# A four-layer graph network on one core: the last layer's attention by seven half-block products, and layernorm's small work moved to GpSimd

## The chip, the core and the metric

The kernel runs on one core of a Trainium2 chip. The core has a matrix engine (TensorE; PE in the profile, with its weight loads as PEld), a vector engine (DVE), an activation engine (ACT), GpSimd (POOL), and SyncE (SP), which here only issues DMAs. Each engine works through its own queue in order; semaphores connect the queues. Matmuls write to PSUM, which GpSimd can't reach; everything else lies in SBUF. The metric is device time in microseconds, a median of several runs.

## The reference

There are 32 graphs of 512 nodes with 256 features each, and four layers, each of the form x = x + layer(relu(layernorm(x)), adj). All four are attentions over the graph's neighbours with different scores. The norm of every layer, and the last layer, which the change rewrites:

```python
h = jnp.maximum(_layernorm(x, axis=-1), 0.0)      # mean, variance, 1/sqrt(v + eps)
...
h = jnp.matmul(feat, W)
Ax = jnp.matmul(h, a_1); Ay = jnp.matmul(h, a_2)
A_xy = jnp.matmul(jnp.matmul(h, a_12), jnp.swapaxes(h, 1, 2))
e = jax.nn.leaky_relu(jnp.swapaxes(Ax, 1, 2) + Ay + A_xy, negative_slope=ALPHA)
e = jnp.where(adj > 0, e, NEG_INF)
attention = jax.nn.softmax(e, axis=-1)
h_out = jnp.matmul(feat, W_1) + jnp.matmul(jnp.matmul(attention, feat), W_2)
return jax.nn.elu(h_out)
```

Layers 1 and 2 have scores of rank one (a leaky sum of a row term and a column term), layer 0 a full product of scores and two convolutions.

## The kernel before, in words

**Tiling.** A graph's 512 nodes are four tiles of 128 partitions. `x`, `y`, `w` and the like are [128, 4, 256] float32, one "page" of 4 KB per partition; there are 34 pages, 8 PSUM banks, 5 buffers for values `v` ([128, 4, 259]), and room for six graphs in flight. Weights of an attention (`e{l}_0` and `e{l}_1`) are two pages of [128, 2, 512]: node tiles 0, 1 and 2, 3 on the partitions, all 512 receivers along the free axis.

**Order.** Nothing loops on the chip. Each piece of work is registered with `op(engine, cost, after, emit, keys...)`: its engine, how long it holds that engine and until when its result lasts (the pair of ns at the top of the file), what it follows, the code that issues it, and the pages and banks that it uses. `Plan.order` then plays all 32 graphs on a model of the engines: whenever an engine is free, it takes the ready operation with the earliest due time, and due times follow from a distance between graphs (one for most, one for the last few), of which the pair with the shortest replay is taken. The instructions are issued in this order, so every engine's queue is fixed in advance and interleaves several layers of several graphs. `SLACK` stretches the costs that the plan reckons with: 1.03 on DVE and ACT, 1.5 on GpSimd.

**Layernorm** (`normed`, lines 552 to 607), for each pair of tiles: DVE takes each tile's statistics (557) and aggregates them to mean and variance (558), adds epsilon (561); GpSimd raises the result to the power -0.5 (564); DVE forms -mean times that (567); ACT normalizes each tile and clips it (571). The tile is then split into 16-bit planes (576), transposed by DMA (579) and joined by ACT (591).

**Products in seven.** Most products of 2 x 2 blocks are already done by seven half-size products in place of eight (`seven`, line 619): bank `p` collects products 1, 6, 7 and 4 one after another, with a copy by ACT or DVE after each, and bank `q` (or the other half of `p`) products 2, 5 and 3, each of which is added to the copy by DVE. Nine such groups run per graph: banks f0, v0, q0, v1, v2, v3, f3, s3, w3. The sums of blocks that they need are formed on DVE (`block_sums`).

**Attention** (`attend`, line 745) is not among them: for two node tiles at a time it runs over the four tiles c of weights, one matmul (758) of 128 x 128 weights against a row of `v`, 257 to 259 columns wide; the last column or columns hold ones, so the product's last column is the sum of the weights. In layer 3 the width is 259. What follows reads the bank: for layer 3 a reciprocal of the sum (1120) and one DVE instruction that scales the product and adds the term `w3` (1125), then the elu and the residual (1131 to 1137) and the store, issued by GpSimd (1154).

**Weights of layers 1 to 3.** Layers 1 and 2 (`leaky_exp_t`): for each of the four tiles ACT forms the leaky sum (732) and the exponential (735), and DVE applies the mask (956, 986). Layer 3: leaky on ACT (1086), a subtraction of the row's shift on DVE (1089), the exponential on ACT (1092), each tile by tile.

Of the kernel before, what the change touches and what calls it, by code (L numbers as in the profile page):

```python
# [38 lines left out]
V_STATS, V_XN, V_TINY, V_TWO = (525.0, 610.0), (322.0, 407.0), (80.0, 165.0), (255.0, 340.0)  # L39
# [3 lines left out]
G_POW, G_STORE = (800.0, 850.0), (900.0, 900.0)  # L43
V_SUM, V_BLOCK = (334.0, 425.0), (790.0, 880.0)
# [162 lines left out]
def kernel(  # L207
# [55 lines left out]
        "w": (pair, F32, "page"), "crest": ([P, 4, N], BF16, "page"),  # L263
        "hs": ([P, 4, N // 2], F32, "page"), "fs": ([P, 4, N // 2], F32, "page"),
# [3 lines left out]
        "st": ([P, NT, 6], F32, None), "mv": ([P, NT, 2], F32, None), "sT": ([P, P], F32, "sT"),  # L268
        "ve": (stat, F32, None), "rstd": (stat, F32, None), "rs": (stat, F32, None), "off": (stat, F32, None),
# [205 lines left out]
    def graph(b, adj_before, x_before):  # L475
# [76 lines left out]
        def normed(l, xs):  # L552
# [3 lines left out]
            def stats(t):  # L556
                nc.vector.bn_stats(T[f"st{l}"][:, t, :], T["x"][:, t, :])  # L557
                nc.vector.bn_aggr(T[f"mv{l}"][:, t, :], T[f"st{l}"][:, t, :])  # L558

            def variance(g):  # L560
                nc.vector.tensor_scalar(T[f"ve{l}"][:, two(g)], T[f"mv{l}"][:, two(g), 1], EPS, None, ALU.add)  # L561

            def root(g):
                nc.gpsimd.tensor_tensor(T[f"rstd{l}"][:, two(g)], T[f"ve{l}"][:, two(g)], mhalf[:, two(g)], ALU.pow)  # L564

            def offset(g):
                nc.vector.scalar_tensor_tensor(T[f"off{l}"][:, two(g)], T[f"mv{l}"][:, two(g), 0], -1.0,  # L567
                                               T[f"rstd{l}"][:, two(g)], ALU.mult, ALU.mult)
# [26 lines left out]
            for g in range(NT // 2):  # L595
# [4 lines left out]
                a = op("V", V_TINY, [a, d], partial(variance, g))  # L600
                r = op("G", G_POW, [a], partial(root, g))
                r = op("V", V_TINY, [r], partial(offset, g))
# [14 lines left out]
        def seven(key, cost, after, keys, work, write, add, beside=0):  # L617
# [16 lines left out]
            def times(x, bank, start, fresh, *wait):  # L634
                return op("PE", cost, after(x) + list(wait), lambda: work(x, T[bank][:, start:], fresh), bank, *keys)
# [69 lines left out]
        def leaky_exp_t(l, vs, sign):  # L705
# [28 lines left out]
            def exp(c):  # L734
                nc.scalar.activation(e(l, c), e(l, c), AF.Exp, scale=sign)  # L735
# [349 lines left out]
        def leaky3(c):  # L1085
            nc.scalar.activation(e(3, c), e(3, c), AF.Prelu, bias=zero, alpha=ALPHA)  # L1086
# [114 lines left out]
```

## Time and profile before

| | us |
|---|---|
| median of 3 runs (2353.06 to 2353.42) | 2353.38 |
| span of the profiled execution | 2353.1 |
| PE busy (granted clock 0.999) | 2328.9 |
| PEld busy | 1992.0 |
| DVE busy | 2099.7 |
| ACT busy | 1719.9 |
| POOL busy | 254.2 |
| layer attention's matmuls, line 758, 4096 instructions, busy | 1017.7 |

The profile is of one execution. Its own time is known only as the span, from the first to the last instruction of the program; it is 0.3 us under the median. Busy time is the union of an engine's instructions. A group's row gives line, engine, operation, the names written and read, the shapes and the count; then busy us, the mean ns of one, and the idle us of the engine just before them, with what ended it. A row of the waits names who waited, for whom, the us in total, how often, and the longest. A row of the chain or of the timeline gives the start in us, the length in us, and what it is. Float32 matmuls appear as two instructions each, and matmuls overlap: one instruction lasts about 165 ns longer than the distance to the next one.

### The profile page before, as it was taken

How to read it: one execution, taken by the hardware profiler on the slowest of the kernel's cores; microseconds unless marked ns; L12 is line 12 of the kernel's file. 1: busy time of each engine (PE TensorE's matmuls, PEld its weight loads, DVE VectorE, ACT ScalarE, POOL GpSimd, SP SyncE). 2: the span in 40 equal slices, each digit the busy share in tenths (PEclk: the TensorE clock that was granted, in tenths of full speed). 3: DMA queues.
4: the chain of work that ended last, by engine and by line, in shares of the span. 5: the costliest groups of instructions: out<-in, count | busy, mean ns of one | idle time of the engine just before them, and what ended most of it. 6: DMA issues, size and time to landing. Idle time of an engine off the chain costs nothing.

```text
span 2353.1 us, 37623 instructions
## 1 busy us (share of the span) xinstructions
PE 2328.9 (99%) x12374; PEld 1992.0 (85%) x12374; DVE 2099.7 (89%) x6060; ACT 1719.9 (73%) x3421; POOL 254.2 (11%) x316
## 2 busy tenths in 40 slices
PE   8999999999999999999999999999999999999998
PEld 5789888888888888888898888888888888888887
DVE  8788899989889898898998889989898988987998
ACT  5677778767787677786777877677776778667874
POOL 3000101111011111011110010100101000010110
PEclk9999999999999999999999999999999999999999
DMA  7431233323333332333323334233343333321221
GB/s 192 106 78 28 57 79 79 88 66 83 72 75 84 78 83 66 70 88 90 82 58 74 80 85 90 54 82 70 88 91 68 86 68 73 86 54 33 55 49 42
DMA packets 429859, 178.26 MB, mean 76 GB/s; under 512 B 384128, under 2 KB 401664, under 8 KB 429664
## 3 DMA queue, kind: packets, MB, share of 16 engines
q1 hardware_dynamic: 424288, 157.51, 31.2%
q0 software_dynamic: 5232, 18.23, 2.4%
q8 instruction: 97, 1.59, 0.3%
q14 instruction: 98, 0.80, 0.1%
q10 hardware_dynamic: 144, 0.13, 0.0%
HBM read 67.64 MB, written 16.89 MB: 36 GB/s over the span
## 4 chain that ended last, share of the span: by engine, by line
PE 94%; DVE 4%; DMA 1%; ACT 1%; issue 0%; POOL 0%; DVEq 0%; ACTq 0%
PE bank_a L758 36%; PE bank_z L918 9%; PE bank_s3p L1040 5%; PE bank_o L936 4%; PE bank_q0p L874 4%; PE bank_f3p L783 4%; PE bank_w3p L809 4%; PE bank_v0p L809 4%; PE bank_f0p L783 4%; PE bank_s3q L1040 3%; PE bank_q0q L874 3%; PE bank_v1p L809 2%; PE bank_v3p L809 2%; PE bank_v2p L809 2%; PE bank_v3q L809 2%; PE bank_v1q L809 2%
## 5 line engine op out<-in xcount | busy, mean ns | idle before, releaser
L758 PE MATMUL bank_a<-v,e 128*128 128x258 f32 (+2 forms) x4096 | 1017.7, 381 | 0.9 <-DVE e L956 0.9
L758 PEld LDWEIGHTS bank_a<-v,e 128*128 128x128 f32 x4096 | 744.1, 190 | 108.9 <-issue 18.2
L591 ACT COPY hT<-planesT 128x512 uint16<-128x512 uint16 x508 | 377.8, 769 | 93.9 <-DMA planesT<-planes 93.2
L564 POOL TENSOR_TENSOR rstd<-ve,mhalf 128x2 f32<-128x2 f32 x256 | 216.0, 863 | 1732.3 <-DVE ve L561 1599.4
L571 ACT ACTIVATE xn<-x,off,rstd 128x256 f32<-128x256 f32 x512 | 278.0, 593 | 39.8 <-DVE off L567 38.9
L918 PE MATMUL bank_z<-e,y 128*128 128x512 f32 x512 | 240.8, 593 | 0.0
L557 DVE BATCH_NORM_STATS2 st<-x 128x6 f32<-128x256 f32 x512 | 210.5, 411 | 3.8 <-DMA x<-in_x_dram 3.8
L576 DVE COPY planes<-xn 128x512 uint16<-128x512 uint16 x380 | 156.4, 420 | 17.3 <-DMA planesT<-planes 10.2
L882 ACT ACTIVATE e<-e 128x512 f32<-128x512 f32 x124 | 77.8, 629 | 121.9 <-DVE e L893 61.8
L732 ACT ACTIVATE e<-row,v 128x512 f32<-128x512 f32 x224 | 156.6, 719 | 0.8 <-DMA row<-row 0.7
L735 ACT ACTIVATE e<-e 128x512 f32<-128x512 f32 x256 | 157.1, 630 | 0.0
L918 PEld LDWEIGHTS bank_z<-e,y 128*128 128x128 f32 x512 | 92.7, 190 | 64.9 <-issue 60.5
L695 ACT COPY v<-bank_v1p 128x258 f32<-128x258 f32 x128 | 47.7, 373 | 120.0 <-PE bank_v1p L809 119.3
L936 PE MATMUL bank_o<-w_sb,zT 128*128 128x256 f32 x512 | 118.5, 379 | 0.2 <-ACT zT L922 0.2
L1047 DVE SCALAR_TENSOR_TENSOR e<-bank_s3p,v,mask 128x256 f32<-128x256 f32 x256 | 111.0, 475 | 8.4 <-PE bank_a L758 4.4
L558 DVE BATCH_NORM_AGGREGATE mv<-st 128x2 f32<-128x6 f32 x512 | 93.2, 182 | 17.5
L936 PEld LDWEIGHTS bank_o<-w_sb,zT 128*128 128x128 f32 x512 | 95.8, 190 | 12.8 <-ACT zT L922 0.6
L664 DVE TENSOR_TENSOR hs<-hT,hs 128x256 f32<-128x256 f32 x254 | 105.1, 414 | 1.1
L667 DVE TENSOR_TENSOR hs<-hT 128x512 f32<-128x512 f32 x127 | 86.6, 682 | 14.5 <-ACT hT L591 14.3
L1086 ACT ACTIVATE e<-e,zero 128x512 f32<-128x512 f32 x128 | 88.2, 721 | 12.9 <-DVE crest L1064 11.4
L885 DVE TENSOR_TENSOR e<-bank_q0p,mask 128x512 f32<-128x512 f32 x124 | 84.5, 682 | 13.8 <-PE bank_q0p L874 12.3
L1089 DVE TENSOR_TENSOR e<-e,crest 128x512 f32<-128x512 f32 x128 | 85.9, 682 | 8.3 <-ACT crest L1083 8.1
(202 smaller groups left out, 4891.3 us busy)
## 6 DMA issues: line engine op xcount, KB each, us to landing
adj<-in_adj_dram SPq DMA_DIRECT2D x128, 256.0 KB
x<-in_x_dram SPq DMA_DIRECT2D x31, 512.0 KB
out_dram<-y POOLq DMA_DIRECT2D x31, 512.0 KB, 3.6
row<-row SPq DMA_DIRECT2D x56, 256.0 KB
planesT<-planes SPq DMA_TRANSPOSE x508
codeT<-code SPq DMA_TRANSPOSE x124
crest<-crest SPq DMA_TRANSPOSE x64
row<-sT SPq DMA_DIRECT2D x56, 2.0 KB
```

What stands on the lines that cost most here:

```text
L557: nc.vector.bn_stats(T[f"st{l}"][:, t, :], T["x"][:, t, :])
L564: nc.gpsimd.tensor_tensor(T[f"rstd{l}"][:, two(g)], T[f"ve{l}"][:, two(g)], mhalf[:, two(g)], ALU.pow)
L571: nc.scalar.activation(T[f"xn{l}"][:, t, :], T["x"][:, t, :], AF.Relu, bias=T[f"off{l}"][:, t : t + 1], scale=T[f"rstd{l}"][:, t : t + 1])
L591: nc.scalar.copy(bits[:, :, :, t * P : (t + 1) * P], T[f"planesT{l}_{t}"].rearrange("p (b c) n -> p b c n", b=2))
L735: nc.scalar.activation(e(l, c), e(l, c), AF.Exp, scale=sign)
L758: nc.tensor.matmul(T[key][:, : LEAD + H + 1 - lead], e(l, c)[:, t * P : (t + 1) * P], T[f"v{l}"][:, c, lead:], start=(c == 0), stop=(c == ...
L783: nc.tensor.matmul(p[:, : N // 2], w[:, x - 1, :], right(x), start=fresh, stop=True, skip_group_check=True)
L809: nc.tensor.matmul(p[:, j * k : (j + 1) * k], right(x)[:, j * P : (j + 1) * P], w[:, x - 1, :], start=fresh and j == 0, stop=True, skip_gr ...
L874: nc.tensor.matmul(p[:, j * N // 2 : (j + 1) * N // 2], right(x)[:, j * P : (j + 1) * P], left(x), start=fresh and j == 0, stop=True, skip ...
L918: nc.tensor.matmul(T[f"bank_z{k}"], T["y0"][:, c, k * P : (k + 1) * P], e(0, c), start=(c == 0), stop=(c == NT - 1))
L936: nc.tensor.matmul(T[key][:, j * H : (j + 1) * H], T["zT"][:, k, t * P : (t + 1) * P], w1_sb[:, k, :], start=(k == 0), stop=(k == HC - 1))
L1040: nc.tensor.matmul(p[:, j * N // 2 : (j + 1) * N // 2], left(x)[:, j * P : (j + 1) * P], right(x), start=fresh and j == 0, stop=True, skip ...
```

## The change

**Layernorm.** The aggregate and the three small instructions on DVE go. GpSimd forms variance, root and offset from the two half-row statistics that `bn_stats` leaves, in ten instructions on [128, 2]:

```diff
             def stats(t):
                 nc.vector.bn_stats(T[f"st{l}"][:, t, :], T["x"][:, t, :])
-                nc.vector.bn_aggr(T[f"mv{l}"][:, t, :], T[f"st{l}"][:, t, :])
...
+            def moments(g):
+                st = T[f"st{l}"][:, two(g), :]
+                gap, total, var, rstd, off = (T[f"{n}{l}"][:, two(g)] for n in ("gap", "sum", "var", "rstd", "off"))
+                gp = nc.gpsimd
+                gp.tensor_tensor(gap, st[:, :, 1], st[:, :, 4], ALU.subtract)
+                gp.tensor_tensor(var, st[:, :, 2], st[:, :, 5], ALU.add)
+                gp.tensor_tensor(gap, gap, gap, ALU.mult)
+                gp.tensor_scalar(var, var, 1.0 / H, EPS, ALU.mult, ALU.add)
+                gp.tensor_scalar(gap, gap, 0.25, None, ALU.mult)
+                gp.tensor_tensor(var, var, gap, ALU.add)
+                gp.tensor_tensor(rstd, var, mhalf[:, two(g)], ALU.pow)
+                gp.tensor_tensor(total, st[:, :, 1], st[:, :, 4], ALU.add)
+                gp.tensor_scalar(total, total, -0.5, None, ALU.mult)
+                gp.tensor_tensor(off, total, rstd, ALU.mult)
...
-                a = op("V", V_TINY, [a, d], partial(variance, g))
-                r = op("G", G_POW, [a], partial(root, g))
-                r = op("V", V_TINY, [r], partial(offset, g))
+                r = op("G", G_CHAIN, [a, d], partial(moments, g))
```

**Weights two tiles at once.** In layers 1 and 2 the exponential and the mask, in layer 3 the leaky pass, the subtraction and the exponential each take a whole page of [128, 2, 512] in one instruction where they took [128, 512]. For example:

```diff
-        def masked1(c):
-            nc.vector.scalar_tensor_tensor(e(1, c), T["codeT"][:, c, :], TINY, e(1, c), ALU.max, ALU.min)
+        def masked1(g):
+            nc.vector.scalar_tensor_tensor(T[f"e1_{g}"], T["codeT"][:, two(g), :], TINY, T[f"e1_{g}"], ALU.max, ALU.min)
```

**Layer 3's attention.** In graphs 0 to 26 (`b < B - 5`) `attend` is replaced by `attend_by_seven`, which forms the block sums of weights (four DVE instructions of 512 columns) and of values (one of 512, two of 256, and a small memset on GpSimd) and hands them to `seven`. Each of the seven products is four matmuls (2 x 2 tiles) of 128 columns; products 3 and 5 take 130, so that the sum of the weights comes out in the last one. New pages: `es3_0`, `es3_1`, `vs3`.

```diff
+            def weights_one():
+                nc.vector.tensor_tensor(T[far][:, 0], weight(1, 0), weight(1, 1), ALU.add)
...
+            def weights_two():
+                nc.vector.tensor_tensor(weight(1, 0), weight(0, 0), T[far][:, 0], ALU.add)
...
+            def work(x, p, fresh):
+                a, b_ = left[x](), right[x]()
+                k = b_.shape[2]
+                for i in range(2):
+                    for j in range(2):
+                        nc.tensor.matmul(p[:, i * WIDE : i * WIDE + k], a[:, j, i * P : (i + 1) * P], b_[:, j, :],
+                                         start=fresh and i == j == 0, stop=True, skip_group_check=True)
...
+            def write(i, f, key, start, after):
+                return op("A", A_HALF, after, lambda: nc.scalar.copy(block(i, f), part(key, start)[:, :, :HALF]), key, f"y{l}")
+
+            def add(i, f, key, start, after):
+                def emit():
+                    nc.vector.tensor_tensor(block(i, f), block(i, f), part(key, start)[:, :, :HALF], ALU.add)
+                    if f == 1:
+                        nc.vector.reciprocal(T[f"rs{l}"][:, two(i)], part(key, start)[:, :, WIDE - 1])
...
-        us = attend(3, es, vs, fourth)
+        if b < B - 5:
+            cs = attend_by_seven(3, [es[0], es[2]], list(vs[0]), [row])
+            us = [op("V", V_PSUM, c + [wb[0, t // 2], wb[1, t // 2]], partial(both_terms_of, t), "y3", "w3")
+                  for t, c in enumerate(cs)]
+        else:
+            us = attend(3, es, vs, fourth)
```

The product is copied to and summed in `y3` in SBUF (four ACT copies, three DVE adds), and `both_terms_of` scales it there and adds `w3`. The plan's costs change with it: statistics alone 340 ns, the GpSimd chain 2200 (lasting 2250), 1024-column passes 1140 on DVE and 960 to 1050 on ACT. `seven` now takes its keys per product.

## The prediction

> **What bounds the kernel now.** I read the page's engine shares first, then three stretches of one graph each from the middle, then who made the tensor engine wait, then the chain that ended last.
>
> ```profile
> span 2353.1 us, 37623 instructions
> PE 2328.9 (99%) x12374; PEld 1992.0 (85%) x12374; DVE 2099.7 (89%) x6060; ACT 1719.9 (73%) x3421; POOL 254.2 (11%) x316
> 602.00:674.00 72.00, 72.00 (x386) 61.97 (x386) 64.36 (x187) 53.48 (x109) 8.06 (x9) 1.00 0.29 64
> 1178.00:1250.00 72.00, 72.00 (x387) 61.98 (x386) 64.29 (x187) 53.17 (x109) 8.04 (x9) 1.00 0.31 63
> ...
> PE bank_n L584 <- ACT xn L571: 8.8, 1, 8.8
> PE bank_f3p L783 <- ACT fa L793: 2.0, 1, 2.0
> PE bank_w3p L809 <- ACT w L1108: 1.9, 1, 1.9
> ```
>
> In the stretches the columns after the length are PE, PEld, DVE, ACT and POOL busy. PE is busy in all 72 us at a granted clock of 1.00; DVE has 7.6 us left per graph, ACT 18.5, POOL 64. The waits of PE are one at the very start (8.8 us) and two of about 2 us near the end; the others add up to under 5 us. So between head and tail **a graph takes as long as the sum of its matmuls**, and PE time taken out is time taken out, as long as nothing else comes late. Busy matmuls overlap (381 ns each in the groups), so their price is read from the chain of waits, where a piece runs to the start of the next:
>
> ```profile
> 622.10 0.45 PE bank_v0p L809 x4
> 649.22 1.74 PE bank_a L758 x8
> 2315.17 1.34 PE bank_w3p L809 x12
> 2334.79 7.87 PE bank_a L758 x36
> ```
>
> A 259-column matmul (last line, layer 3) costs 7.87/36 = 218.6 ns; a 128-column one, with its own weight load, 1.34/12 = 111.7 ns (0.45/4 = 112 in the first).
>
> **The change, part by part.** (a) *Attention of layer 3, graphs 0 to 26.* Each f32 matmul is two instructions, as the group row shows (4096 for 2048 calls). Out go 16 calls = 32 instructions of 259 columns: 32 x 218.6 = 6995 ns. In come 7 products x 4 calls x 2 = 56 instructions, 40 of 128 and 16 of 130 columns. The 130-column form is not in the trace: below it lies 111.7 (128 columns), above it 113.5 (111.7 plus two columns at 218.6/259 = 0.84). I take 112.5, between them. 40 x 111.7 + 16 x 112.5 = 6268. That is 0.73 us per graph, **27 x 0.73 = 19.6 us**. Bounds: with 111 for all 21.0; with 113.5 for all 17.3. Weight loads rise by 24 per graph, but the 128-column products of the v and w banks have the same one load per 128 columns and run at the 112 used.
>
> The seven products go one after another through bank p, each waiting for ACT's copy (about 0.37 us), and bank q for DVE's adds. What hides this is the work of other graphs and layers: nine such chains per graph run in the trace already (f0, v0, q0, v1, v2, v3, f3, s3, w3), and PE still has no gap. Cover gone, a chain would show some six waits of 0.5 us, 3 us per graph.
>
> (b) *DVE.* The rows:
>
> ```profile
> L557 DVE BATCH_NORM_STATS2 st<-x 128x6 f32<-128x256 f32 x512 | 210.5, 411 | 3.8 <-DMA x<-in_x_dram 3.8
> L558 DVE BATCH_NORM_AGGREGATE mv<-st 128x2 f32<-128x6 f32 x512 | 93.2, 182 | 17.5
> L561 DVE TENSOR_SCALAR ve<-mv 128x2 f32<-128x2 f32 x256 | 37.6, 159 | 0.0
> L567 DVE SCALAR_TENSOR_TENSOR off<-mv,rstd 128x2 f32<-128x2 f32 x256 | 37.3, 151 | 1.5 <-POOL rstd L564 1.3
> L1089 DVE TENSOR_TENSOR e<-e,crest 128x512 f32<-128x512 f32 x128 | 85.9, 682 | 8.3 <-ACT crest L1083 8.1
> ```
>
> Out per graph, in busy time: 16 aggregates x 0.18, 8 variances x 0.16, 8 offsets x 0.15, 4 reciprocals x 0.16 = 6.0 us. Twelve 512-column weight passes (layers 1 to 3) become six of 1024: the columns stay, six starts go. A start costs 682 - 2 x (682 - 414) = 146 ns (414 is the 256-column sum of line 664), 0.9 us. In come five 512-column sums (0.68), two of 256 (0.42), three PSUM adds (0.42), two reciprocals: 5.8 us. **Net -1.1 us per graph, and -6.3 in the last five** (which keep the reciprocals). DVE isn't the bound in the middle, so this is worth nothing there, but it doesn't cost either: 63.3 of about 71.3 us.
>
> (c) *ACT.* Twelve exponentials and four leaky passes are joined in twos (eight starts gone, about 0.1 us each by the same working), four copies of 0.37 us come: +0.7 us against 18.5 idle. Nothing.
>
> (d) *Layernorm's small work.* POOL's one power per pair of tiles becomes ten instructions, 80 per graph, and DVE's queue waits for POOL no more; ACT's norm (line 571) waits for POOL directly. Behind the chain in POOL's queue stand other graphs' chains and the store of y3. The power's price depends on what DVE does:
>
> ```profile
> 613.93 1.34 POOL L564 TENSOR_TENSOR rstd<-ve,mhalf 128x2 f32<-128x2 f32 x2 [21.14 <-DVE ve L561]
> 648.95 0.69 DVE L1009 SCALAR_TENSOR_TENSOR x<-y,x 128x512 f32<-128x512 f32 x1
> 649.12 1.07 POOL L564 TENSOR_TENSOR rstd<-ve,mhalf 128x2 f32<-128x2 f32 x1 [7.73 <-DVE ve L561]
> ...
> 880.12 0.68 DVE L1076 TENSOR_REDUCE top<-crest 128x4 bf16<-128x512 bf16 x1
> 880.29 0.69 POOL L564 TENSOR_TENSOR rstd<-ve,mhalf 128x2 f32<-128x2 f32 x1 [7.37 <-DVE ve L561]
> ```
>
> Beside an idle DVE, or a reduction with one input, it takes 0.67 to 0.69; issued 0.17 us into a sum of two SBUF tensors, 1.07, ending 0.55 after that sum ends. The group's mean is 863 ns, so on average 0.18 us are waiting. The DVE sum keeps its 0.69: the delay is POOL's alone. The Trainium skill ("SBUF — State Buffer", Who interferes with whom) speaks against this part: GpSimd shares a port pair with VectorE, a VectorE instruction with two SBUF inputs contends with a GpSimd one that reads SBUF, and the second to issue fully blocks; the rows agree. By the rule at its worst, each of the ten behind a whole 0.6 us sum, a chain would take over 6 us (an estimate); the sum here goes by the mean wait in the rows.
>
> The nine small POOL instructions are not in the trace. Below: 0.10 us (a memset, 95 to 100 ns). Above: 0.28 (the 128-column select that makes the identity) + 0.18 waiting = 0.46. I take the middle, 0.28. Chain: 0.86 + 9 x 0.28 = **3.4 us, between 1.8 and 5.0**. Before, aggregate to offset took 0.18 + 0.16 + 0.86 + 0.15 = 1.35. So a norm comes some 2 us later, the second pair of a layer 4 if both come together; POOL is busy 28 of 71 us. The plan orders the queues as if the chain lasted 2250 x 1.5 = 3.4 us, so ACT's queue should not find it late. A memset of 0.1 us per graph (line `edge`) joins POOL's queue. In the middle the other graphs in flight hide the chain. Not hidden in the head: the first PE work waits for the first norm, before any other graph is there: +0.5 to +3, I take 2. In the tail PE's two waits end a stretch (2254 to 2270 us in the chain) that runs through DVE, aggregates and variances among it; relief there (up to 4 us) against four longer norms in the last graph (up to 6) and tiles that come in twos: -4 to +6, I take +1. Scattered waits in the middle: 0 to 3, I take 1.
>
> **Sum.** The profiled execution spans 2353.1, 0.3 below the median of 2353.4. 2353.4 - 19.6 + 2 + 1 + 1 = **2337.8**; bounds by the terms -21.0 - 3.5 and -17.3 + 12: 2329 to 2348.
>
> **Rivals.** *Tail relief* (0.10): DVE's lighter queue in the last graphs removes the two 2 us waits and nothing else moves: 2353.4 - 20.5 - 3 + 2 = 2332. For it: the chain there is DVE, line after line. Against: the norms' longer way lies on the same chain.
>
> *Eaten by the seven* (0.10): the chain through bank p finds too little other work, 0.6 us of PE wait per graph. 27 x 0.6 = 16: 2353. For it: the 32 old instructions stood in no such chain, and the new ones hold three more of the 34 pages. Against: nine such chains run without a gap.
>
> *GpSimd's queue* (0.17), slower: norms in ACT's order wait for chains. Place: line 571's queue on ACT. A chain later than planned by d stops ACT for d, eight times per graph; ACT has 18.6 us idle, so it decides from 8d = 18.6, d = 2.3, a chain of 5.7 us (0.54 per small instruction). At 6.0 it costs 8 x 2.6 - 18.6 = 2.2 us per graph, 32 x 2.2 = 70: 2353 + 70 - 16 = 2407. For it: the power itself has a mean of 0.86, and at that price POOL would be full (8 x 8.6 of 71). Against: memsets and the select take 0.1 to 0.28 on the same engine.
>
> **How the numbers follow.** Forecast 0.63, tail relief 0.10, eaten 0.10, GpSimd's queue 0.17. A measurement tells 0.2% (4.7 us) from no change, so faster means under 2348.7, slower over 2358.1: 0.73, 0.10, 0.17. The range takes in the first three with their bounds and the near edge of the fourth: 2329 to 2360.
>
> **What would show it.** Right: in a middle stretch PE still busy throughout with a graph every 71.3 us; 130-column rows at about 112 ns in the chain; a POOL chain of 3 to 4 us, POOL near 40% busy; DVE near 89%. Wrong: ACT's norm waiting for POOL by hundreds of us in total, or PE waiting for line 571's successors; PE waiting at the new products' copies; a head longer by over 3 us; small POOL instructions near 0.5 us.

## The result, and the profile after

| | before | after |
|---|---|---|
| median, us | 2353.22 | 2433.32 |
| ratio, 95% interval | | **1.0341** [1.0326, 1.0356] |
| span of the profiled execution, us | 2353.1 | 2436.3 |
| sum of PE's matmul spacings at their usual length, us | 2317.0 | 2297.2 |
| what is left: PE's waits and slowed spacings, us | 20.6 | 123.9 |

The changed kernel is 3.4% slower; the forecast was 2337.8 us, 0.7% faster. The last two rows are worked out from the trace: for each form of matmul the usual distance to the next one, summed over all; what is left of the distances is waiting, and some spacing at a lower clock (see the price of PE's gaps, below). The matmul time fell by 19.8 us, and the rest rose by 103.3. The profile of the changed kernel, engine shares and the two stretches that the prediction showed (columns: length, then PE, PEld, DVE, ACT, POOL busy, clock, DMA):

```profile
span 2436.3 us, 40134 instructions
PE 2346.8 (96%) x13022; PEld 2010.0 (83%) x13022; DVE 2078.5 (85%) x5060; ACT 1720.7 (71%) x3273; POOL 943.7 (39%) x2647
```

```profile
602.00:674.00 72.00, 68.51 (x377) 58.47 (x376) 61.00 (x150) 49.30 (x92) 35.35 (x102) 0.98 0.32 74
1178.00:1250.00 72.00, 69.94 (x385) 59.67 (x385) 61.25 (x151) 49.98 (x94) 27.54 (x73) 0.95 0.31 67
```

PE is no longer busy throughout, and no other engine is either: DVE has 61 of 72 us, ACT 49, POOL 28 to 35. Nothing is full, so something is late. PE's waits of the changed kernel (us in total, times, longest) name many engines, for a few us each:

```profile
PE bank_f0p L881 <- DVE fa L896: 23.2, 15, 2.5
...
PE bank_n L592 <- ACT xn L579: 9.5, 1, 9.5
...
PE bank_a3p L842 <- ACT y L852: 5.8, 6, 2.1
```

These are the last links only. ACT's own waits, of the kernel before and of the changed one, show what comes ahead of them:

```profile
ACT xn L571 <- DVE off L567: 38.9, 34, 5.5
```

```profile
ACT xn L579 <- POOL off L576: 222.9, 127, 6.2
```

The norm waited 39 us for the offset; it now waits 223 us for the last instruction of GpSimd's chain, in 127 of 512 norms. One such case in the changed kernel's chain of waits (start, length, what):

```profile
616.93 0.71 POOL var L570
...
618.65 0.78 POOL rstd L573
...
619.98 0.50 POOL off L576
...
620.53 0.58 ACT xn L579
621.11 0.66 ACT hT L599
...
623.87 2.79 PE bank_z L1016 x4
```

GpSimd's instructions, the power and the offset among them, stand on the chain one after another, then the norm, then what ACT has queued behind it, then a PE that stood idle. POOL has 18% of the chain that ended last.

### The profile page after: what moved, and what is told of

Read it like the earlier page. It is cut to its first block, busy times and chain, and to the rows that moved or that the text cites. A ratio compares the mean times of both kernels' runs of the same rounds, so it can differ in the third digit from the quotient of the medians.

```text
span 2436.3 us, 40134 instructions
## 1 busy us (share of the span) xinstructions
PE 2346.8 (96%) x13022; PEld 2010.0 (83%) x13022; DVE 2078.5 (85%) x5060; ACT 1720.7 (71%) x3273; POOL 943.7 (39%) x2647
## 4 chain that ended last, share of the span: by engine, by line
PE 59%; POOL 18%; DVE 13%; ACT 5%; issue 4%; DMA 1%; POOLq 0%; DVEq 0%; SPq 0%; ACTq 0%
PE bank_a L765 16%; PE bank_z L1016 7%; PE bank_o L1034 4%; POOL rstd L573 4%; PE bank_f3p L881 3%; PE bank_q0p L972 3%; PE bank_a3p L842 3%; PE bank_s3p L1140 3%; PE bank_s3q L1140 3%; PE bank_v0p L907 3%; PE bank_f0p L881 2%; PE bank_a3q L842 2%; PE bank_q0q L972 2%; POOL gap L567 2%; POOL gap L571 2%
## 5 line engine op out<-in xcount | busy, mean ns | idle before, releaser
L765 PE MATMUL bank_a<-v,e 128*128 128x258 f32 (+2 forms) x3232 | 827.6, 383 | 5.6 <-DVE e L1054 2.3
L765 PEld LDWEIGHTS bank_a<-v,e 128*128 128x128 f32 x3232 | 585.9, 192 | 82.9 <-issue 7.4
L567 POOL TENSOR_TENSOR gap<-st 128x2 f32<-128x2 f32 x256 | 97.8, 382 | 1175.7 <-DVE st L561 1146.8
L573 POOL TENSOR_TENSOR rstd<-var,mhalf 128x2 f32<-128x2 f32 x256 | 212.0, 828 | 20.1
L584 DVE COPY planes<-xn 128x512 uint16<-128x512 uint16 x380 | 155.8, 419 | 23.8 <-ACT xn L579 13.3
L742 ACT ACTIVATE e<-e 128x1024 f32<-128x1024 f32 x128 | 136.8, 1069 | 0.6
L1054 DVE SCALAR_TENSOR_TENSOR e<-codeT,e 128x1024 f32<-128x1024 bf16 x64 | 78.3, 1223 | 49.6 <-ACT e L742 49.3
L702 ACT COPY v<-bank_v3p 128x258 f32<-128x258 f32 x128 | 47.7, 373 | 96.9 <-PE bank_v3p L907 96.8
L881 PE MATMUL bank_f0p<-hs,att_s 128*128 128x256 f32 x248 | 76.2, 390 | 30.0 <-DVE fa L896 23.2
L1038 DVE SCALAR_TENSOR_TENSOR z<-bank_o,rs,b_sb 128x256 f32<-128x256 f32 x128 | 57.4, 479 | 49.5 <-PE bank_o L1034 47.4
L1186 ACT ACTIVATE e<-e,zero 128x1024 f32<-128x1024 f32 x64 | 73.3, 1150 | 35.9 <-DVE crest L1164 35.6
```

Source lines behind the costliest of these rows:

```text
L567: gp.tensor_tensor(gap, st[:, :, 1], st[:, :, 4], ALU.subtract)
L573: gp.tensor_tensor(rstd, var, mhalf[:, two(g)], ALU.pow)
L584: (nc.scalar.copy if l in BYACT else nc.vector.tensor_copy)(T[f"planes{l}_{t}"], bits)
L765: nc.tensor.matmul(T[key][:, : LEAD + H + 1 - lead], e(l, c)[:, t * P : (t + 1) * P], T[f"v{l}"][:, c, lead:], start=(c == 0), stop=(c == ...
L881: nc.tensor.matmul(p[:, : N // 2], w[:, x - 1, :], right(x), start=fresh, stop=True, skip_group_check=True)
```

## The experiments

The theory (theory 1 in the expectations): the norms come late because GpSimd's chain of ten is long, and every other part of the change does what was forecast. Rivals: the new order of the queues, the products in seven or the passes over two tiles cost the time themselves; or DVE's relief and load decide. Later runs ask in which way a late norm costs (ACT standing still; the last tile alone; the first pairs' small room; the two pairs of a layer in series). Unless it is said otherwise, all queues keep the changed kernel's order and only what an operation emits is changed. Each ratio is to the kernel before, with its 95% interval.

### Is it the chain?

**chain_of_two** keeps of the ten the power and one product, on unscaled statistics; variance, mean and epsilon are left out:

```diff
-                gp.tensor_tensor(gap, st[:, :, 1], st[:, :, 4], ALU.subtract)
...
-                gp.tensor_tensor(off, total, rstd, ALU.mult)
+                nc.gpsimd.tensor_tensor(rstd, st[:, :, 2], mhalf[:, two(g)], ALU.pow)
+                nc.gpsimd.tensor_tensor(off, st[:, :, 1], rstd, ALU.mult)
```

> The changed kernel with the same costs in the plan, so the same order of every queue, but of GpSimd's ten instructions per pair of tiles only two are issued (a power and a product on the raw statistics); the other eight are left out, so the normalization isn't the reference's. Theory 1 (GpSimd's chain lasts 4.05 us on average and up to 7.1, where the plan allowed 3.4, and ACT's norms and then the matmuls wait for it): the chain falls to about 1.3 us, ACT's 223 us of waiting for it go, 2335 to 2345 us. Theory 2 (the seven products of layer 3 wait for their copies and pages): 2425 to 2440 us, as the changed kernel. Theory 3 (the new order is worse whatever the chain takes): 2425 to 2440 us too.

Measured: 2336.29 us, 0.9923 [0.9906, 0.9939]. Its engine shares and the first stretch:

```profile
PE 2310.2 (99%) x13022; PEld 1999.2 (86%) x13022; DVE 2077.5 (89%) x5060; ACT 1720.7 (74%) x3273; POOL 328.9 (14%) x599
```

```profile
602.00:674.00 72.00, 72.00 (x417) 62.86 (x416) 66.17 (x162) 54.18 (x106) 7.80 (x18) 1.00 0.39 87
```

PE is full again, with 417 matmul instructions in 72 us where the changed kernel had 377, and the same order, products and passes. All of the loss, 97 us, is the eight instructions more on GpSimd; everything else in the change gains 17 us.

**chain_of_six** leaves out the two scalings, epsilon, and the sum of means and its scaling.

```diff
-                gp.tensor_scalar(var, var, 1.0 / H, EPS, ALU.mult, ALU.add)
-                gp.tensor_scalar(gap, gap, 0.25, None, ALU.mult)
...
-                gp.tensor_tensor(total, st[:, :, 1], st[:, :, 4], ALU.add)
-                gp.tensor_scalar(total, total, -0.5, None, ALU.mult)
-                gp.tensor_tensor(off, total, rstd, ALU.mult)
+                gp.tensor_tensor(off, st[:, :, 1], rstd, ALU.mult)
```

> The changed kernel, every queue in the same order, with six of GpSimd's ten instructions per pair of tiles: the scalings, epsilon and the sum of the two means are left out, so the normalization isn't the reference's. Two instructions gave 2336 us, ten 2433. Theory 1, with a threshold (it costs where the chain outlasts the 3.4 us that the plan allowed; six should last about 2.5 us, seldom over 3.8): 2337 to 2352 us. Theory 1 without a threshold (each instruction on GpSimd costs its share, 97/8 = 12 us): about 2385 us.

Measured: 2334.96 us, 0.9922 [0.9907, 0.9937]: four instructions more than in the run before cost nothing. In the trace the chains are twice as long as with two (2.36 us on average against 1.21), and yet in seven of the eight pairs of a graph the norm starts within 0.1 us of where it started there (medians; the eighth, layer 2's first pair, 0.3 us later). The cost isn't in proportion to the chain; it sets in between six and ten.

**chain_of_nine** orders the sums so that one scaling goes, with the same result:

```diff
-                gp.tensor_tensor(gap, st[:, :, 1], st[:, :, 4], ALU.subtract)
+                gp.tensor_tensor(total, st[:, :, 1], st[:, :, 4], ALU.add)
...
+                gp.tensor_scalar(total, total, -0.5, None, ALU.mult)
-                gp.tensor_scalar(gap, gap, 0.25, None, ALU.mult)
+                gp.tensor_tensor(gap, st[:, :, 1], total, ALU.add)
+                gp.tensor_tensor(gap, gap, gap, ALU.mult)
```

> The changed kernel, same order, with the same moments in nine GpSimd instructions, arranged so that neighbours depend on each other less often (the half difference is formed as mean of one half minus the mean). Undisturbed the chain should last about 2.5 us in place of 2.9, its mean about 3.5 in place of 4.05. Six instructions (mean 2.4) gave 2335 us, ten 2433. Theory 1 with a threshold near 3.4 us: between, 2365 to 2405 us.

Measured: 2398.38 us, 1.0192 [1.0177, 1.0207]. From the first instruction's start to the offset's end a chain took on average 4.05 us with ten, 3.80 with nine, 2.36 with six. A quarter of a microsecond per chain, between ten and nine, is worth 35 us of time.

### Other queues, other passes

**ten_in_old_order** takes the kernel before, with its order, and puts all ten instructions in the place of the power; the aggregate and the small work on DVE go. Nothing else is changed.

```diff
-                nc.vector.bn_aggr(T[f"mv{l}"][:, t, :], T[f"st{l}"][:, t, :])
...
             def root(g):
-                nc.gpsimd.tensor_tensor(T[f"rstd{l}"][:, two(g)], T[f"ve{l}"][:, two(g)], mhalf[:, two(g)], ALU.pow)
+                gp.tensor_tensor(gap, st[:, :, 1], st[:, :, 4], ALU.subtract)
...
+                gp.tensor_tensor(off, total, rstd, ALU.mult)
```

> The kernel before, every queue in its old order, with the ten GpSimd instructions issued where its one power was, and the aggregate, variance and offset on DVE gone; attention and passes as before. The plan allowed the power 1.3 us and the offset 0.2; ten should last some 3.6. Theory 1: late by some 2 us each time, 2400 to 2500 us though DVE has less to do. Theory 2 (the cost is the attention's): 2340 to 2355 us.

Measured: 2375.35 us, 1.0093 [1.0078, 1.0108]: slower, but by 22 us, less than was expected of it (a miss by 25 us). In this order a pair's norm stood a median 5.5 us behind its statistics in the kernel before; in the changed kernel's order, when the chain is short (chain_of_two), 4.5. So the order sets how much lateness is free. But the chains were shorter here too, 3.53 us on average against 4.05; how much of the smaller loss is due to each isn't shown.

**narrow_passes** issues each pass over two tiles as two instructions of 512 columns again (on ACT and DVE, layers 1 to 3):

```diff
         def shifted(g):
-            nc.vector.tensor_tensor(T[f"e3_{g}"], T[f"e3_{g}"], shift().unsqueeze(1).to_broadcast([P, 2, N]), ALU.subtract)
+            for c in (2 * g, 2 * g + 1):
+                nc.vector.tensor_tensor(e(3, c), e(3, c), shift(), ALU.subtract)
```

> The changed kernel, same order, with each pass over two tiles issued as two instructions of 512 columns again. Theory 1 says that GpSimd's reads wait out DVE's instructions with two SBUF inputs; these now hold the port 0.6 us at a time in place of 1.2: the chain's mean falls from 4.05 to about 3.8 us and the time to 2395 to 2425 us, although DVE and ACT have six and eight starts more per graph. If the width doesn't matter: 2430 to 2445 us.

Measured: 2420.02 us, 1.0283 [1.0268, 1.0298]. The time came down by 13 us, into the range expected of it, but not for the reason given there: the mean chain stayed at 4.03 us (nine tenths were under 5.57, against 5.87). The passes over two tiles are not what makes the chains long: the slowest of them, the second pair of layer 1, still takes a median 6.09 us against 6.37 (below). Where the 13 us come from isn't shown.

**aggregate_back** puts the aggregate back on DVE and leaves GpSimd four instructions:

```diff
                 nc.vector.bn_stats(T[f"st{l}"][:, t, :], T["x"][:, t, :])
+                nc.vector.bn_aggr(T[f"mv{l}"][:, t, :], T[f"st{l}"][:, t, :])
...
+                gp.tensor_scalar(var, mv[:, :, 1], EPS, None, ALU.add)
+                gp.tensor_scalar(total, mv[:, :, 0], -1.0, None, ALU.mult)
                 gp.tensor_tensor(rstd, var, mhalf[:, two(g)], ALU.pow)
                 gp.tensor_tensor(off, total, rstd, ALU.mult)
```

> The changed kernel, same order, with the aggregate on DVE again and four instructions on GpSimd (epsilon, the negative mean, the power, the offset). The chain should last about 1.8 us; DVE has 2.9 us more per graph than the plan knows, 68.9 of 71.3. Theory 1: 2337 to 2352 us, below both kernels, with some waits for DVE at the upper end. If DVE's late statistics cost as much as GpSimd's chain: 2360 to 2400 us.

Measured: 2380.62 us, 1.0117 [1.01, 1.0134], 29 us above theory 1's range and inside the one for late statistics on DVE: the chain fell to 1.80 us and the time did not follow. Its engine shares and the first stretch:

```profile
PE 2331.0 (98%) x13022; PEld 1994.5 (84%) x13022; DVE 2138.5 (90%) x5572; ACT 1717.5 (72%) x3273; POOL 463.3 (19%) x1111
```

```profile
602.00:674.00 72.00, 70.39 (x399) 60.47 (x399) 66.56 (x175) 54.13 (x106) 14.72 (x38) 1.00 0.34 77
```

DVE is busy 61 us more than in chain_of_two over the whole run, PE has gaps, and DVE isn't full in this stretch (66.6 of 72 us, against 66.2 in chain_of_two, which gets more done in them). Late offsets are not the reason. The offset is ready 1.8 to 3.1 us after the statistics (medians by layer and pair), in every pair before the moment at which the norm starts in chain_of_two (2.3 to 7.4 us), and the norm waits for it as long as in chain_of_six, which takes 46 us less; the rows of chain_of_six and of aggregate_back:

```profile
ACT xn L575 <- POOL off L572: 55.7, 36, 5.3
```

```profile
ACT xn L574 <- POOL off L571: 54.8, 36, 5.1
```

So the cost is the aggregates' time on DVE, which this order, planned without them, does not have to give, though DVE is idle a tenth of the time.

### How a late norm costs

**norms_later** asks whether ACT's standing still is the price. After the order is found, each norm is moved up to two places down ACT's queue, so that ACT works on other things in the meantime (on average 1.4 places).

```diff
     order, took = plan.best(POOLS)
+    order = norms_later(order, 2)
```

> The changed kernel with the ten instructions, and in ACT's queue each norm put behind up to two of the instructions that followed it, wherever the other queues' orders allow it (1.4 places on average); the other engines' queues keep their order. Theory 1a (what costs is that ACT's queue stands still behind a norm that waits, with the copies that free the matmuls' banks behind it): 2385 to 2415 us. Theory 1b (the norm itself comes too late for the products that need it, whatever ACT does meanwhile): 2430 to 2450 us.

Measured: 2459.24 us, 1.0446 [1.043, 1.0461]: slower than the changed kernel. ACT waits for POOL only 72 us in total, and the waiting has gone one engine on, to the split of the norm on DVE (the same row had 13.3 us in the changed kernel):

```profile
DVE planes L584 <- ACT xn L579: 116.6, 92, 7.5
```

**norms_later_four** (up to four places) and **norms_later_nine** (two places, the chain of nine) complete it.

```diff
-    order = norms_later(order, 2)
+    order = norms_later(order, 4)
```

> As norms_later, with up to four places (2.3 on average). Theory 1a: 2360 to 2395 us. Theory 1b: 2435 to 2460 us.

> norms_later's order of ACT (up to two places) with the chain of nine: the reference's result with most of the lateness gone. Theory 1a: 2345 to 2375 us; theory 1b: as chain_of_nine or slower.

Measured: 2528.32 us, 1.0741 [1.0725, 1.0757], and 2450.38 us, 1.0416 [1.0398, 1.0433]. ACT's standing still isn't the price: the norm's own lateness is, whoever has to wait for it. These runs make it later (layer 0's first norm, for one, starts 9.0 us after its statistics in norms_later and 6.0 in the changed kernel), and the time goes up by 26 and 95 us over the changed kernel, and by 52 over chain_of_nine.

**four_at_once** does one chain of ten for all four tiles at the second pair's place, wherever the order has that ahead of the first norm (93 of 128 layers), so GpSimd's work nearly halves; **four_at_once_nine** with nine.

```diff
             def moments(g):
-                st = T[f"st{l}"][:, two(g), :]
+                if joined.get((b, l)):
+                    if g == 0:
+                        return
+                    ts = slice(0, NT)
...
+                st = T[f"st{l}"][:, ts, :]
```

> The changed kernel, every queue in the same order and the reference's result, but where no norm stands between a layer's two chains of ten (93 of the 128 layers) the first is left out and the second does all four tiles, on 128x4. The second pair's chain then no longer waits for the first's in GpSimd's queue; the first pair's waits for the second pair's statistics. Theory 1b (what counts is when the layer's last tile is normed, since the block sums need all four): the last chain ends some 3 us earlier, 2340 to 2390 us. If the first pair's lateness decides: 2430 to 2460 us.

> The same with the chain of nine. Theory 1b: 2336 to 2370 us, perhaps below the kernel before; otherwise near chain_of_nine's 2398 us or above.

Measured: 2443.90 us, 1.0385 [1.037, 1.0401], and 2428.94 us, 1.0319 [1.0302, 1.0337]. POOL is busy 646.9 us in place of 943.7 and the time is no better: so half the work on GpSimd is no help by itself. The first pair's norm now waits for the second pair's statistics too: in the trace of four_at_once it starts 1 to 2.9 us later than in the changed kernel (medians by layer; in layer 1 6.97 us after its own statistics, 4.09 before). That this lateness makes up for what the shorter queue saved is likely, and only argued.

### Which norms

Three runs give the chain of two to some layers only and leave the other layers ten.

```diff
                 gp = nc.gpsimd
+                if l in (0, 1):
+                    gp.tensor_tensor(rstd, st[:, :, 2], mhalf[:, two(g)], ALU.pow)
+                    gp.tensor_tensor(off, st[:, :, 1], rstd, ALU.mult)
+                    return
```

> The changed kernel, same order, with GpSimd's chain cut to two instructions in layer 2 alone (its normalization isn't the reference's), ten elsewhere. In the run with two everywhere the time from a pair's last statistics to its first norm shows how much room the order leaves: a median of 5.7 us for the first pair of layer 0, 4.1 in layer 1, 2.3 in layer 2, 3.6 in layer 3, and 4.5 to 7.4 for the second pairs; an undisturbed chain of ten takes 2.9, the mean one 4.05. Theory 1c (the cost falls where the room is shorter than the chain): layer 2 gives back half or more of the 97 us, 2360 to 2390 us. If every chain costs alike, a quarter: 2409 us.

> The same with the short chain in layer 3 alone. Theory 1c: a fifth to two fifths of the 97 us come back, 2395 to 2415 us. Every chain alike: 2409 us.

> The same with the short chain in layers 0 and 1, where the room is the longest. Theory 1c: 10 to 35 us come back, 2398 to 2425 us. Every chain alike: half, 2384 us.

Measured: layer 2 alone 2422.57 us, 1.0288 [1.0273, 1.0303]; layer 3 alone 2399.82, 1.0203 [1.0186, 1.0219]; layers 0 and 1 together **2347.72, 0.9974 [0.9964, 0.9983]**. Of the 97 us, 11 and 33 come back for layers 2 and 3, and 86 for layers 0 and 1; these are 130 together, so the layers' losses are not independent. The trace of two_in_3 shows one link: a layer 0 chain often stands directly behind a layer 3 chain of another graph, and with layer 3's short, layer 0's second offset is ready at 6.97 us after its statistics in place of 8.54. It had been expected the other way round, from the small room of the first pairs in layers 2 and 3; that theory fell.

**short_where_tight**, made on the fallen theory, keeps the whole result: nine instructions, and DVE's aggregate for the first pairs of layers 2 and 3.

```diff
+                if (l, t // 2) in ((2, 0), (3, 0)):
+                    nc.vector.bn_aggr(T[f"mv{l}"][:, t, :], T[f"st{l}"][:, t, :])
```

> A version with the reference's result: the chain of nine, except for the first pairs of layers 2 and 3, where DVE aggregates again (0.9 us per graph) and GpSimd issues four instructions. Theory 1c: 2345 to 2375 us, against 2398 for nine everywhere; below the kernel before only if layers 0 and 1 cost next to nothing.

Measured: 2401.78 us, 1.0204 [1.0189, 1.0219], no better than nine everywhere (2398.38).

Single chains in the trace show another pattern. For layers 0 and 1, medians over graphs 2 to 28 in us, counted from the end of the pair's last statistics: when its chain starts in the changed kernel, how long the chain itself takes, when the offset is ready and the norm starts, and when the norm starts in chain_of_two, where hardly anything is late ("room").

| layer, pair | chain starts | chain takes | offset ready | norm starts | room |
|---|---|---|---|---|---|
| 0, first | 1.62 | 4.23 | 5.71 | 5.99 | 5.68 |
| 0, second | 3.56 | 4.87 | 8.54 | 8.64 | 7.41 |
| 1, first | 0.08 | 3.58 | 3.67 | 4.09 | 4.05 |
| 1, second | 2.25 | 6.37 | 8.65 | 8.69 | 5.86 |

In layer 1 the second pair's chain stands directly behind the first's in all 27 graphs and so starts 2.25 us late. It also meets most of DVE's sums: 4.3 us of DVE instructions with both inputs in SBUF run during it (median; 0.1 to 2.3 in the other pairs), and it takes 6.37 us. Together that is 8.65 against a room of 5.86. Two runs test the series: they shorten only the first pair of layers 0 and 1, or only the second.

```diff
                 gp = nc.gpsimd
+                if (l, g) in ((0, 0), (1, 0)):
+                    gp.tensor_tensor(rstd, st[:, :, 2], mhalf[:, two(g)], ALU.pow)
+                    gp.tensor_tensor(off, st[:, :, 1], rstd, ALU.mult)
+                    return
```

> Only the first pair of tiles of layers 0 and 1 has a chain of two instructions (the power and the product, on unscaled statistics; variance, scalings, epsilon and the mean are left out there); the other six chains per graph have ten. Theory (in layers 0 and 1 the second pair's chain stands behind the first's, and the two together exceed the room): the second pair's norm gets its 2.8 us back though its own chain is as long as before, and most of the 86 us that both pairs gave come back: 2345 to 2375 us. Rival (each chain's own length decides, whatever stands before it): about what the first pairs alone are late for, 0 to 0.3 us of lateness against 1.2 to 2.8: 2415 to 2433 us. Rival (only the sum of GpSimd's work counts): half of the 86 us: 2385 to 2395.

> Only the second pair of tiles of layers 0 and 1 has a chain of two instructions (work left out as in the run beside it); the first pairs keep ten. Theory (two chains in series): the pair is as much shorter as in the run beside it, so the time is about the same as there, 2345 to 2375 us, and the two runs lie within 20 us of each other. Rival (each chain's own length decides): the second pairs were the late ones, so nearly all comes back here, 2345 to 2355, and next to nothing in the run beside it. Rival (only the sum of GpSimd's work counts): 2385 to 2395 in both.

Measured: first pairs 2354.79 us, 1.0005 [0.9995, 1.0014]; second pairs 2355.92 us, 1.0007 [0.9998, 1.0016]. The two agree within 1.2 us, and each alone returns 77 to 79 of the 97 us. Both rivals are out: each chain's own length had 2415 us or more for the first run, and the sum of GpSimd's work 2385 to 2395 for both. In the first of them the late norms still have a chain of ten; with the chain ahead of it gone, layer 1's second offset is ready at 5.48 us, and in the second run at 4.88: both under the room of 5.86, and its norm starts at 6.02 in both, against 8.69. Either of the two in series was enough to take away.

### A whole result with a shorter chain

**chain_of_seven** computes all of the norm in seven instructions: one product of the statistics with a table of constants, one sum of both halves (which gives -mean, half the gap, the variance's part and epsilon side by side), the square, two sums, the power, the offset.

```diff
+                halves = st.rearrange("p t (h s) -> p (t h) s", h=2).unsqueeze(2).to_broadcast([P, 4, 2, 3])
+                gp.tensor_tensor(mparts.rearrange("p t h (c s) -> p (t h) c s", c=2), halves,
+                                 mcoef.rearrange("p t h (c s) -> p (t h) c s", c=2), ALU.mult)
+                gp.tensor_tensor(mboth, mparts[:, :, 0, :], mparts[:, :, 1, :], ALU.add)
+                gp.tensor_tensor(mboth[:, :, 4], mboth[:, :, 4], mboth[:, :, 4], ALU.mult)
+                gp.tensor_tensor(rstd, mboth[:, :, 4], mboth[:, :, 2], ALU.add)
+                gp.tensor_tensor(rstd, rstd, mboth[:, :, 3], ALU.add)
+                gp.tensor_tensor(rstd, rstd, mhalf[:, two(g)], ALU.pow)
+                gp.tensor_tensor(off, mboth[:, :, 1], rstd, ALU.mult)
```

> The whole result with seven GpSimd instructions in place of ten: one multiplication of the four half-row statistics by a constant table (24 elements per partition), one sum of the two halves (12), the square, two sums, the power, the offset. The order of every queue is that of the changed kernel. Theory (a chain costs nothing until chains in series exceed the room of 5.9 to 7.4 us): a mean chain of about 2.8 us, two in series 5.6, so nearly nothing is lost: 2335 to 2352 us, under both kernels. Rival (the cost goes with the length: 2335 us at 2.36, 2398 at 3.80): 2354 us at 2.8, between 2350 and 2362. Rival (a wider table instruction is slow on GpSimd, the chain stays at 3.5 us or more): 2380 us or more.

Measured: **2348.01 us, 0.9976 [0.9966, 0.9986]**: 85 us under the changed kernel and below the kernel before by 0.24%, a small gain, but one whose interval leaves out 1. The mean chain is 3.23 us, longer than the 2.8 expected; a line from 2.36 us (2335) to 3.80 (2398) would put it at 2373, so the time again does not go with the length. Engine shares and the new instruction's group, then the norm's wait:

```profile
PE 2312.7 (99%) x13022; PEld 1996.0 (85%) x13022; DVE 2076.1 (89%) x5060; ACT 1720.4 (73%) x3273; POOL 739.5 (32%) x1885
L576 POOL TENSOR_TENSOR mparts<-st,mcoef 128x24 f32<-128x24 f32 x256 | 83.9, 328 | 1276.1 <-DVE st L569 1247.0
```

```profile
ACT xn L586 <- POOL off L583: 103.9, 67, 6.2
```

ACT still waits 104 us for POOL, and PE is busy 99% of the span. The total of a wait is not its price: the norm of layer 1's second pair starts 6.30 us after its statistics, against a room of 5.86, and that is nearly in time.

## Why the prediction was wrong

**(a) The products in seven: right.** 19.6 us were forecast, and the matmul spacings sum to 19.8 less. The prices in the changed kernel's chain of waits, two pieces of layer 3's products:

```profile
630.55 0.89 PE bank_a3p L842 x8
...
638.41 0.90 PE bank_a3q L842 x8
```

That is 111 to 112 ns for each of the eight instructions; over all unstalled ones the 130-column form has 111.8 (112.5 assumed). The copies and adds between the products are hidden as forecast: PE waited 5.8 us in all for the copy (line 852, shown above), and chain_of_two has every product in seven and a full PE. The rival "eaten by the seven" is out.

**(b) DVE: relief too large in the sum, its worth too small.** Forecast were -1.1 us for each of 27 graphs and -6.3 for each of five, 61 us; DVE's busy time fell by 21 (2099.7 to 2078.5). The sum of the instructions' durations did fall by 53, nearer the forecast; but durations overlap their neighbours', and the busy time counts what they cover. DVE's timeline in the changed kernel shows how:

```profile
610.69 0.15 DVE L1004 RECIPROCAL rs<-bank_a 128x1 f32<-128x1 f32 x1
610.76 0.40 DVE L561 BATCH_NORM_STATS2 st<-x 128x6 f32<-128x256 f32 x1
```

The reciprocal "lasts" 0.15 us and the next instruction starts 0.07 us after it. In the kernel before, the distance from the start of one to the start of the next was 107 ns on average for an aggregate, 76 for a variance and 81 for an offset, about half of the 182, 159 and 151 ns of their rows. And "DVE isn't the bound in the middle, so this is worth nothing there" fails: with the aggregates back the time is 2380.62 us, against 2334.96 with a chain of six that is longer. An engine that had a tenth of its time left was not free in this order, and late offsets were not the reason (aggregate_back). What an order planned with the aggregates would give was not measured.

**(c) ACT: right in effect, not in size.** +0.7 us per graph was forecast, and taken for nothing; over the run that is some +14 us (27 graphs with the copies, five without). Busy time rose by 0.8, from 1719.9 to 1720.7 us.

**(d) The chain: the step that failed.** "Chain: 0.86 + 9 x 0.28 = 3.4 us, between 1.8 and 5.0" was low but inside its bounds: 4.05 us on average, 3.75 the median, 5.87 at nine tenths. The prices of the small instructions were about right. GpSimd's groups in the changed kernel:

```profile
L573 POOL TENSOR_TENSOR rstd<-var,mhalf 128x2 f32<-128x2 f32 x256 | 212.0, 828 | 20.1
L567 POOL TENSOR_TENSOR gap<-st 128x2 f32<-128x2 f32 x256 | 97.8, 382 | 1175.7 <-DVE st L561 1146.8 <-DVE rs L1066 27.6
...
L570 POOL TENSOR_SCALAR var<-var 128x2 f32<-128x2 f32 x256 | 69.5, 272 | 21.7
```

The nine small ones take 272 to 382 ns, 0.32 on average, where 0.28 was taken; that is 0.3 us of the 0.65 us missing, and the rest is the 0.07 us of issue between dependent ones, which the chain shows as steps of its own. The sum also took the waiting behind DVE by its mean and lost its spread. The chain of layer 1's second pair in graph 13, 6.2 us long, shows where it goes; GpSimd's timeline, then DVE's:

```profile
945.23 0.19 POOL L570 TENSOR_SCALAR var<-var 128x2 f32<-128x2 f32 x1
945.50 1.36 POOL L571 TENSOR_SCALAR gap<-gap 128x2 f32<-128x2 f32 x1
...
948.19 1.06 POOL L575 TENSOR_SCALAR sum<-sum 128x2 f32<-128x2 f32 x1
```

```profile
945.50 1.29 DVE L1238 SCALAR_TENSOR_TENSOR y<-r,x 128x512 f32<-128x512 f32 x2
...
947.95 1.23 DVE L1085 SCALAR_TENSOR_TENSOR e<-codeT,e 128x1024 f32<-128x1024 bf16 x1
```

A scaling of two columns takes 0.19 us by itself and 1.36 beside two sums of layer 3's elu in a row, 1.06 beside a mask of 1024 columns; each ends 0.07 us after the DVE work that it met. The chain's first instruction (line 567) took 1.50 us behind three in a row (two of line 1232, then one of line 671, each with both inputs in SBUF). The Trainium skill's "SBUF — State Buffer", Who interferes with whom, has this: a GpSimd instruction that reads SBUF is fully blocked by a VectorE one with two SBUF inputs that got there first. The trace agrees, and shows that a second and a third sum right behind the first can be let through as well.

The step that decided was the next: "The plan orders the queues as if the chain lasted 2250 x 1.5 = 3.4 us, so ACT's queue should not find it late", and "In the middle the other graphs in flight hide the chain". Both failed. The norms have a room, fixed by the order, of 2.3 to 7.4 us by layer and pair. Chains in series, the second of them drawn out by DVE's sums, fill more than that in layers 0 and 1 (in layer 1's second pair 8.65 us against 5.86), and what the queues hold for a norm in time is late with it: ACT's norm waited 223 us in all for GpSimd, one of the signs of being wrong that the prediction had named. The hint was in the prediction ("the second pair of a layer 4 if both come together") and was not put against any room. What a plan told the chain's real length would give was not measured.

**The rival "GpSimd's queue"** was right in its kind: named as slower, by norms that wait for GpSimd, with 70 us. Its point of decision was wrong: 5.7 us of chain, from ACT's average idle time of 18.6 us per graph. The loss came at 4.05 us, and the place where it is counted isn't ACT's queue (norms_later). Idle time on average says nothing about the one moment at which an instruction is due.

**The price of PE's gaps** was missing too: a wait of 2 us costs more than 2 us. The changed kernel's chain about such a gap, and two stretches around it:

```profile
1225.12 1.61 PE bank_a3p L842 x8
...
1230.10 0.89 PE bank_a3p L842 x8
```

```profile
1210.00:1225.00 15.00, 13.06 (x66) 9.36 (x65) 11.67 (x28) 11.57 (x24) 10.46 (x23) 1.00 0.40 70
1225.00:1229.00 4.00, 3.88 (x11) 2.42 (x12) 2.89 (x5) 4.00 (x8) 0.00 (x0) 0.58 0.43 86
```

PE idles for 2.06 us before the first line. Then eight 128-column instructions take 1.61 us, where they take 0.89 five us later, and the granted clock is 0.58 over these 4 us. The trace's clock records show what that is made of: stretches of 3.41 us at half clock. Before the end of the run the changed kernel has 15 of them, each starting within 1.4 us of the end of a PE gap of 1.86 to 2.71 us (two gaps of 2.06 and 2.11 us have none); the kernel before has one, behind a gap of 2.01 us. In them matmul spacings at about half speed took some 22 us more than usual, 2 us in the kernel before: about 20 of the 103 us.

**Head and tail.** The first PE work waited 9.5 us for its norm, 8.8 before: +0.7, where +2 was taken. The tail was not measured by itself.

**What stays open.** Layers 0 and 1 account for most of the loss, and chains in series are shown by the two runs there; how far the 11 and 33 us of layers 2 and 3 are their own norms' or pass through layer 0 is not. No run has an order planned for the ten instructions alone, or for the old norm beside the new attention. Nor is it shown why narrow_passes gained 13 us, nor whether layer 3's scaling (line 1245), which now reads `y3` in SBUF where it read PSUM, adds to the meetings: no run took it away.

## What to carry to other kernels

When small work moves to an otherwise idle engine, don't set its length against that engine's idle time or the waiting engine's average idle time: take, for each consumer, the distance in the trace between its input's producer and its start, and put all chains that queue ahead into the sum. A queue order fixed in advance hid lateness up to about that distance for nothing and handed on what went beyond; what helped here was to shorten the dependent sequence (fewer, wider instructions), and moving the consumer back only moved the wait. The total of a wait row isn't its price: 104 us of it stood beside a full tensor engine (chain_of_seven), and 55 both beside one with gaps (aggregate_back) and beside the fastest run (chain_of_six).

## What the runs showed of the hardware

- A GpSimd instruction on [128, 24] takes about as long as one on [128, 2] (328 ns on average in chain_of_seven, against 272 to 382 in the changed kernel): at these sizes the cost is the instruction, hardly its elements. So seven instructions, some of them wider, took 3.23 us where ten took 4.05.
- DVE's durations don't show that it meets GpSimd: layer 3's subtraction of 1024 columns takes 1.18 to 1.23 us in all 64 cases, 53 of them with a GpSimd instruction beside it, while a GpSimd instruction beside DVE's sums goes from 0.19 to over 1 us.
- The granted clock was 0.58 over 4 us after PE had idled 2.06 us, and fell to half after 15 gaps of 1.86 to 2.71 us in all. The Trainium skill's "TensorE: Matmul & The Clock Gate", Why this matters for your kernels, asks for no gaps above about 3 us; here shorter ones were enough.
